# Two convolution norms' moments moved from VectorE to ScalarE, two product blocks moved from GpSimd to VectorE, and one more block folded before its transposes

## The chip, the cores and the metric

The kernel runs on one core of a Trainium2 chip. The metric is device time in microseconds of one execution, the median over runs. The core's engines run their own instruction queues in order and meet through semaphores: TensorE (PE, with its weight loads as PEld), VectorE (DVE), ScalarE (ACT), GpSimd (POOL) and the queue that issues most transfers (SP). Each engine starts an instruction only when the one ahead of it in its queue has been issued and when its own waits are met, so one late wait holds all that stands behind it.

## The reference, cut to what matters

A decoder layer with three sublayers, each followed by a residual and a layer norm, over x of 16 batches, 256 positions and 512 features:

```python
x = _layernorm(x + attention(x, w_q, w_k, w_v, w_o))          # 16 heads, causal, ternary weights
x = _layernorm(x + convolution(ctx, ctx, x, ssm_kernel, D))   # the part that is changed
x = _layernorm(x + feed_forward(x, gamma, W))                 # RMS norm, 8-bit rows, ternary W

def convolution(k, v, q, ssm_kernel, D):          # 32 heads of 8 channels, L = 512
    kv = einsum('bhil,bhjl->bijhl', k, v)         # all 64 products of two channels of a head
    y = causal_convolution(kv, ssm_kernel)        # along l, by a transform of length 1024
    out = y + kv * D
    return einsum('bijhl,bhil->bjhl', out, q)     # weighed by the queries and summed over i
```

Here k and v are both the context, so the product of channels i and j is that of j and i, and only the distances d = j - i from 0 to 4 (modulo 8, half of distance 4) have to be multiplied: 4 x 128 + 64 = 576 columns for 8 channels by 16 batches.

## The kernel before, in words

The first half of the time is attention for 16 batches, software-pipelined by `step`; nothing in it changes. The second half is the loop over the 32 heads `h` of the convolution, `for h in range(XH)` at line 1071, and a tail, `last_heads`, at line 987. Both are written out in an order by hand: the calls are made in the order in which each engine gets its instructions, so the order of the calls in the loop body is the order of every queue.

What one pass of the loop does, for head `h` and the heads before and after it:

- `load` (line 735) fetches, two heads ahead, the head's context `c` and a matrix `w` of shifted filter taps. `multiply` (line 942, through `prepare`, line 739) makes the products `kv` of head h + 1. Distance k takes columns k x 128 to (k + 1) x 128, and distance 4, half as wide, the last 64. GpSimd multiplies distances 1, 2, 4 and 3 (distance 4 together with 2); ScalarE squares for distance 0 (`square`, line 760).
- `products` (line 785) is the convolution as matrix products: position block `lb` of four takes lb + 1 blocks of taps, two halves of 288 columns each. Its result `y` fills two PSUM banks, and there are two such buffers, so a block may be computed while VectorE still reads the one before it, but not two blocks ahead. Below, P0 to P3 are the products of blocks 0 to 3.
- `with_queries` (lines 797 to 812) is VectorE's five instructions that multiply a block of `y` by the queries `q`, into `own` and `turn`. Below, Q0 to Q3.
- `add` (lines 960 and 962) is GpSimd's sum of `own` and `turn`, eight parts into four; for the blocks in `FOLDED` it then folds four parts into two. Below, A0 to A3 with F1 to F3; block 0 is not folded before the change.
- `read` (line 968, with `total` at line 817) transposes the parts of a block and sums them in PSUM into `tok`: two transposes for a folded block, four for block 0. Ten transposes a head.
- For head h - 1 the finished `tok` is normalised. `second_moments` takes mean and variance by `moments2` (line 833): `bn_stats`, `bn_aggr`, and one small instruction for each quarter of a shifted variance, all on VectorE. `engine_roots`, `newton` and `inverse_roots` (lines 843 to 863) turn a quarter into a reciprocal root, partly on ScalarE. `second_centred` and `second_max` (lines 878 and 882) prepare the 8-bit rounding; `second_norm` (line 884) makes the normalised `x2` and the rounded rows `fi`; `turn` (line 900) transposes these by a transfer.
- For head h - 2, `feed_product` (line 907) multiplies by the ternary weights and `feed_forward` (line 909) adds the residual into `r3` and takes its moments, again by `moments2`. For head h - 3, `finish` (line 914) normalises `r3` and sends it out.
- `copy` (lines 772 and 773) is ScalarE's copy of the queries of head h + 1, which Q0 of that head needs.

So VectorE's queue has, in one pass: Q0, Q1, the moments of `tok`, `second_centred`, a reciprocal, `second_max`, Q2, a reciprocal and six small instructions, `r3` and its moments, Q3. GpSimd's has A3 and F3 of the head before, distance 1, A0, distances 2 and 4, A1, F1, distance 3, A2, F2. TensorE's has P0, `read` of block 2 of the head before, P1, `read` of block 3 of the head before, P2, `feed_product`, `read` of block 0, P3, `read` of block 1.

In the tail, `last_heads`, the last head's norm, the feed-forward products of the last two heads and three output norms follow each other with nothing of the loop left to lie beside them.

Of the kernel before, what the change touches and what calls it, by code (L numbers as in the profile page):

```python
# [9 lines left out]
F32 = mybir.dt.float32  # L10
# [5 lines left out]
P = 128  # L16
# [16 lines left out]
def decoder_kernel(ctx: ExitStack, tc: tile.TileContext, x, ctx_t, w_q, w_k, w_v, w_o, ker, d_skip, gamma, w_f, out):  # L33
# [151 lines left out]
    def rounded(pool, tag, t):  # L185

        xi = pool.tile([P, E], BF16, name=f"{tag}_i", tag=f"{tag[:2]}_i")
        nc.scalar.activation(xi, t, AF.Copy, bias=-MAGIC)
        return xi
# [539 lines left out]
    with ExitStack() as l2:  # L729
# [2 lines left out]
        ps_y = l2.enter_context(tc.tile_pool(name="ps_y", bufs=2, space=PSUM, side="right"))  # L732
        pb = l2.enter_context(tc.tile_pool(name="pb", bufs=1, side="right"))
        gam = pb.tile([P, E], F32, name="gam")
        op = l2.enter_context(tc.tile_pool(name="op", bufs=4, side="right"))


# [3 lines left out]
        def prepare(h):  # L741


            c = lp.tile([P, NB, EXT, B], F32, name="c")
            nc.sync.dma_start(c[:, :, 0:XD, :], ctx_t[h])
            nc.sync.dma_start(c[:, :, XD:EXT, :], ctx_t[h][:, :, 0 : EXT - XD, :])

            w = lp.tile([P, E], F32, name="w")
            nc.sync.dma_start(w, bass.AP(taps.tensor, taps.offset + h * (E + P), [[1, P], [1, E]]))

            kv = cp.tile([P, NB, NPAIR], F32, name="kv")

            def part(at, n, i, d):
                nc.gpsimd.tensor_tensor(  # L754
                    kv[:, :, at : at + n * B].rearrange("p c (i b) -> p c i b", b=B),
                    c[:, :, i : i + n, :], c[:, :, i + d : i + d + n, :], ALU.mult,
                )

            def square():
                nc.scalar.activation(  # L760
                    kv[:, :, 0:P].rearrange("p c (i b) -> p c i b", b=B), c[:, :, 0:XD, :], AF.Square
                )

            def multiply(k):
                part(k * P, XD, 0, k)
                if k == 2:
                    part(4 * P, 4, 0, 4)

            q = cp.tile([P, NB, EXT, B], F32, name="q")

            def copy(c=slice(0, NB)):
                nc.scalar.copy(q[:, c, 0:XD, :], x1t[:, h, c])
                nc.scalar.copy(q[:, c, XD:EXT, :], x1t[:, h, c, 0 : EXT - XD, :])

            return w, kv, q, multiply, copy, square

        FOLDED = (1, 2, 3)
        Y0 = E - HALF

        def products(lb, w, kv):  # L780
# [50 lines left out]
        FORMS = ((1.0, LN_EPS), (1.0, LN_EPS), (1.0 + RMS_EPS, RMS_EPS * LN_EPS))  # L831

        def moments2(src, roots, forms):
            st = sm.tile([P, 6], F32, name="st2")
            nc.vector.bn_stats(st, src)
            mv = sm.tile([P, 2], F32, name="mv2")
            nc.vector.bn_aggr(mv, st)
            for i in forms:
                a, b = FORMS[i]
                nc.vector.tensor_scalar(roots.quarter[:, i : i + 1], mv[:, 1:2], a / 4, b / 4, ALU.mult, ALU.add)  # L840
            return mv[:, 0:1]

        def engine_roots(roots):
            c = roots.cols
            nc.scalar.activation(roots.root[:, c], roots.quarter[:, c], AF.Sqrt)  # L845
# [18 lines left out]

        def shifted(mean, res):
            shift = sm.tile([P, 1], F32, name="shift")
            nc.vector.tensor_scalar(shift, mean, res, -1.0, ALU.mult, ALU.mult)
            return shift

        def second_moments(m, roots):  # L870
# [4 lines left out]

        def second_centred(m):
            m.xn = fp.tile([P, E], F32, name="xn")
            nc.vector.scalar_tensor_tensor(m.xn, m.flat, m.mean, gam, ALU.subtract, ALU.mult)

        def second_max(m):  # L880
            m.amax = sm.tile([P, 1], F32, name="amax2")
# [2 lines left out]
        def second_norm(m, roots):  # L884
            rstd, both = (roots.res[:, i : i + 1] for i in (1, 2))
            shift = shifted(m.mean, rstd)
            m.x2 = fp.tile([P, E], F32, name="x2")
            nc.scalar.activation(m.x2, m.flat, AF.Identity, bias=shift, scale=rstd)
            amax = m.amax
            nc.vector.tensor_scalar(amax, amax, both, 1e-5, ALU.mult, ALU.add)  # L890
            mul = sm.tile([P, 1], F32, name="mul2")
            nc.vector.reciprocal(mul, amax)
            nc.vector.tensor_scalar(mul, mul, both, 127.0, ALU.mult, ALU.mult)
            m.inv = sm.tile([P, 1], F32, name="inv2")
            nc.vector.tensor_scalar(m.inv, amax, w_inv[:, 4:5], 1.0 / 127.0, ALU.mult, ALU.mult)
            m.ft = fp.tile([P, E], F32, name="fq_t", tag="q_t")
            nc.scalar.activation(m.ft, m.xn, AF.Copy, bias=MAGIC, scale=mul)
            m.fi = rounded(fp, "fq", m.ft)

        def turn(m):  # L900
            m.fit = fp.tile([P, NB, P], BF16, name="fit")
# [37 lines left out]
        def square(m):  # L939
            m.inputs[5]()  # L940

        def multiply(m, k):
            m.inputs[3](k)

        def copy(m, *blocks):
            m.inputs[4](*blocks)
# [73 lines left out]
        with tc.manual_schedule(engines=by_hand):  # L1020
            load(first_head, 0)
            load(heads[1], 1)
            nc.sync.dma_start(gam, gamma.partition_broadcast(P))
            multiply(first_head, 1)
            multiply(first_head, 2)
            acc = {0: turn_sums(m, 0)}
            divide_sums(m)
            acc[1] = turn_sums(m, 1)
            keep(k, B - 3, (1,))
            m.ots, m.last = {}, {}  # L1030
            for t in range(NT):
                divide(m, t, acc[t])
                out_scales(m, slice(t, t + 1))
                m.ots[t] = scaled(ap, f"oq{t}", m.o[:, t, :], m.mul_o[t])
                if t == 0:
                    moments(n)
            multiply(first_head, 3)
            square(first_head)
            m.oit = kp.tile([P, NT, NB, P], BF16, name="oit")
            transposed(ps, m.oit[:, 0], rounded(ap, "oq0", m.ots[0]))  # L1040
            close(m, slice(0, 1))
            transposed(ps, m.oit[:, 1], rounded(ap, "oq1", m.ots[1]))
            normalize(n)
            moments_one(m, 0)
            keep(n, B - 2, (0,))
            multiplied(first_head, 0)
            normalize_one(m, 0)
            keep(m, B - 1, (0,))
            copy(first_head, slice(0, 1))
            copy(first_head, slice(1, NB))  # L1050
            block(first_head, 0)
            close(m, slice(1, 2))
            moments_one(m, 1)
            multiplied(first_head, 1)
            block(first_head, 1)
            normalize_one(m, 1)
            keep(n, B - 2, (1,))
            multiplied(first_head, 2)
            keep(m, B - 1, (1,))
            l1.close()  # L1060
            fp = l2.enter_context(tc.tile_pool(name="fp", bufs=2))
            sm = l2.enter_context(tc.tile_pool(name="sm", bufs=3))
            ps_k = l2.enter_context(tc.tile_pool(name="ps_k", bufs=2, space=PSUM))
            ps2 = l2.enter_context(tc.tile_pool(name="ps2", bufs=2, space=PSUM))


            def roots_for(h):
                return roots_of(slice(0 if h > 2 else 1, 3))

            ahead = roots_for(0)  # L1070
            for h in range(XH):
                roots, ahead = ahead, roots_for(h + 1)

                on(load, h + 2, h + 2)
                on(add, h - 1, 3)
                on(block, h, 0)
                on(read, h - 1, 2)
                on(multiply, h + 1, 1)
                on(square, h + 1)

                on(block, h, 1)
                on(add, h, 0)
                on(read, h - 1, 3)
                on(multiply, h + 1, 2)
                on(second_moments, h - 1, roots)
                if h > 0:
                    engine_roots(roots)
                on(second_centred, h - 1)
                if h > 0:
                    newton(roots)  # L1090
                on(second_max, h - 1)

                on(block, h, 2)
                on(feed_product, h - 2)
                if h > 0:
                    inverse_roots(roots)
                on(add, h, 1)
                on(read, h, 0)
                on(multiply, h + 1, 3)
                on(second_norm, h - 1, roots)  # L1100
                on(turn, h - 1)
                on(finish, h - 3, roots, h - 3)
                on(copy, h + 1)
                on(feed_forward, h - 2, ahead)

                on(block, h, 3)
                on(add, h, 2)
                on(read, h, 1)
            last_heads(ahead)
# [37 lines left out]
```

## Time and profile before

| What | us |
|---|---|
| median of three runs (862.62 to 864.34) | 863.07 |
| the profiled execution, its own time | 861.76 |
| its span | 860.0 |
| mean granted TensorE clock | 0.988 |
| TensorE busy | 803.8 |
| VectorE busy | 690.5 |
| GpSimd busy | 583.4 |
| ScalarE busy | 427.0 |

The profiled execution's own time is the span and 1.76 us that lie around it; it is 1.31 us under the median. Busy shares over the whole span mix attention with the loop over heads. In the stretch from 500 to 800 us, which holds nothing but the loop, TensorE is 99% busy, GpSimd 93%, VectorE 88% and ScalarE 42%, and one head takes 12.40 us. A busy TensorE isn't proof of a TensorE at its limit, since matmul ends are modelled: a short wait can be hidden in a row.

In the views below, "<-" after a square bracket's number names what ended the idle time before an instruction; a group of equal instructions on one line has the time from the first one's start to the last one's end.

### The profile page before, as it was taken

The numbers are of one execution on the slowest core, as the hardware profiler recorded it, in microseconds if no ns is written. First come the engines' busy times: TensorE is split into PE (matmuls) and PEld (weight loads), VectorE is DVE, ScalarE is ACT, GpSimd is POOL, SyncE is SP. The second block draws the span as 40 slices with busy tenths as digits, with TensorE's granted clock in tenths as the row PEclk, the third lists the DMA queues.
The fourth block names the chain that finished last, engine by engine and source line by source line (L and its number), as shares of the span: only waits on it lengthen the run. The fifth ranks groups of instructions, "written<-read, shape, count | busy, mean of one in ns | idle before, by whom it ended". The sixth has DMA issues, their size and how long they took to land.

```text
span 860.0 us, 20228 instructions
## 1 busy us (share of the span) xinstructions
PE 803.8 (93%) x7754; PEld 555.9 (65%) x7754; DVE 690.5 (80%) x1889; ACT 427.0 (50%) x707; POOL 583.4 (68%) x652
## 2 busy tenths in 40 slices
PE   4889999999999999998878999999999999999993
PEld 3556666666666666665646767776777677777762
DVE  6757887788888778876666888988898889888885
ACT  6555655556565555655644334433443444344434
POOL 5265544545454454544639999999999999999980
PEclk9999999999999999999979999999999999999997
DMA  9111222333122222211320233223323332333211
GB/s 319 45 33 53 66 69 69 75 76 76 26 63 68 71 75 76 51 39 35 88 65 19 69 99 95 71 81 99 88 67 91 99 84 68 95 98 74 75 38 55
DMA packets 102207, 64.51 MB, mean 75 GB/s; under 512 B 66464, under 2 KB 83104, under 8 KB 102112
## 3 DMA queue, kind: packets, MB, share of 16 engines
q1 hardware_dynamic: 102112, 63.23, 27.5%
q8 instruction: 61, 1.00, 0.5%
q14 instruction: 34, 0.28, 0.1%
HBM read 43.34 MB, written 8.47 MB: 60 GB/s over the span
## 4 chain that ended last, share of the span: by engine, by line
PE 77%; DVE 10%; ACT 6%; issue 4%; POOL 2%; DMA 0%; ACTq 0%; DVEq 0%; POOLq 0%
PE y L785 32%; PE s L341 6%; PE acc L293 6%; PE s L381 5%; ACT p L386 4%; PE tok L820 4%; PE pv L409 4%; PE s L334 4%; PE acc_o L482 3%; DVE nmax L346 3%; PE acc_f L907 3%; PE sums L416 2%; PE s L374 2%; PE acc_v L311 2%; PE tp L528 1%
## 5 line engine op out<-in xcount | busy, mean ns | idle before, releaser
L785 PE MATMUL y<-kv,w 128*128 128x288 f32 x1280 | 335.0, 409 | 4.4 <-DVE turn L812 2.0
L785 PEld LDWEIGHTS y<-kv,w 128*128 128x128 f32 x1280 | 234.0, 191 | 64.9 <-PE tok L820 10.5
L960 POOL TENSOR_TENSOR own<-own,turn 128x512 f32<-128x512 f32 x127 | 161.7, 1274 | 21.1 <-DVE turn L812 11.0
L390 POOL TENSOR_SCALAR_AFFINE_SELECT p<-p 128x512 f32<-128x512 f32 x128 | 81.3, 659 | 139.5 <-ACT p L386 129.1
L754 POOL TENSOR_TENSOR kv<-c 128x512 f32<-128x512 f32 (+1 forms) x128 | 144.4, 1140 | 2.9 <-PE sums L416 2.9
L346 DVE TENSOR_REDUCE nmax<-s 128x4 f32<-128x512 f32 (+1 forms) x128 | 116.5, 952 | 35.5 <-PE s L341 35.5
L386 ACT ACTIVATE p<-s 128x1536 f32<-128x1536 f32 x64 | 92.9, 1452 | 70.3 <-PE s L381 70.2
L845 ACT ACTIVATE root<-quarter 128x3 f32<-128x3 f32 (+2 forms) x34 | 7.0, 204 | 159.5 <-DVE quarter L840 159.5
L396 POOL TENSOR_TENSOR both<-p 128x512 f32<-128x512 f32 x64 | 82.3, 1286 | 5.3
L797 DVE SCALAR_TENSOR_TENSOR own<-y,q 128x128 f32<-128x128 f32 x128 | 36.7, 286 | 50.5 <-PE y L785 42.6
L962 POOL TENSOR_TENSOR own<-own 128x256 f32<-128x256 f32 x95 | 69.1, 727 | 7.5
L293 PE MATMUL acc<-xit,w 128*128 128x256 bf16 x504 | 68.9, 276 | 3.6 <-DVE w L158 3.4
L800 DVE TENSOR_TENSOR own<-y,q 128x384 f32<-128x384 f32 x128 | 70.1, 548 | 0.0
L803 DVE TENSOR_TENSOR turn<-y,q 128x384 f32<-128x384 f32 x128 | 70.1, 548 | 0.0
L820 PEld LDWEIGHTS tok<-ident,own 128*128 128x128 f32 x318 | 37.7, 141 | 38.5 <-POOL own L962 26.0
L293 PEld LDWEIGHTS <-w 128*128 128x128 bf16 x512 | 45.9, 99 | 24.1 <-issue 8.5
L820 PE MATMUL tok<-ident,own 128*128 128x128 f32 x318 | 58.7, 283 | 2.4 <-issue 1.2
L341 PE MATMUL s<-kt,qt 32*128 32x128 f32 (+1 forms) x1024 | 60.0, 348 | 0.0
L381 PE MATMUL s<-qt,kt 32*128 32x256 f32 (+1 forms) x1024 | 57.4, 335 | 0.0
L409 PE MATMUL pv<-p,va 128*32 128x256 f32 (+1 forms) x1024 | 54.9, 332 | 0.0
L421 ACT COPY ot<-pv 128x256 f32<-128x256 f32 x64 | 23.9, 373 | 50.8 <-PE pv L409 50.2
L334 PE MATMUL s<-mask,ident_h 128*128 128x256 bf16 x256 | 38.3, 271 | 11.0 <-ACT p L386 9.9
(148 smaller groups left out, 1359.8 us busy)
## 6 DMA issues: line engine op xcount, KB each, us to landing
xt<-in_x SPq DMA_DIRECT2D x16, 512.0 KB, 4.1
xr<-in_x SPq DMA_DIRECT2D x16, 512.0 KB, 4.6
c<-in_ctx_t SPq DMA_DIRECT2D x32, 256.0 KB, 3.3
w<-taps SPq DMA_DIRECT2D x32, 256.0 KB, 4.1
out_y<-res SPq DMA_DIRECT2D x31, 256.0 KB, 2.3
c<-in_ctx_t SPq DMA_DIRECT2D x32, 128.0 KB, 3.2
x1t<-in_w_q SPq DMA_DIRECT2D x1, 1024.0 KB, 6.6
x1t<-in_w_k SPq DMA_DIRECT2D x1, 1024.0 KB, 9.4
```

The source lines that it names most:

```text
L293: nc.tensor.matmul(acc[:, j, :], w[:, c, o * P : (o + 1) * P], m.xit[:, c].rearrange("p t k -> p (t k)"), start=(c == 0), stop=(c == NB - 1),)
L341: nc.tensor.matmul(s[:, r, lo:hi], m.qt[rows, g, q0 : q0 + P], m.kt[rows, g, 0:nk], start=False, stop=True, skip_group_check=True,)
L346: nc.vector.tensor_reduce(m.nmax[:, t, :, g], s[:, :, cols], AX.X, ALU.max, negate=True)
L381: nc.tensor.matmul(s[:, r, lo:hi], m.kt[rows, g, k0 : k0 + P], m.qt[rows, g, q0:S], start=False, stop=True, skip_group_check=True,)
L386: nc.scalar.activation(p, s[:, :, 0 : 3 * P], AF.Exp)
L390: nc.gpsimd.affine_select(out=own, in_=own, compare_op=ALU.is_ge, fill=0.0, base=0, pattern=[[0, 4], [1, P]], channel_multiplier=-1,)
L396: nc.gpsimd.tensor_tensor(both, p[:, :, P : 2 * P], p[:, :, 2 * P : 3 * P], ALU.add)
L409: nc.tensor.matmul(acc[rows, q0:S], m.va[:, j, 4 * g + r, :], p[:, r, src], start=(j == 0), stop=(j == 1), skip_group_check=True, tile_pos ...
L754: nc.gpsimd.tensor_tensor(kv[:, :, at : at + n * B].rearrange("p c (i b) -> p c i b", b=B), c[:, :, i : i + n, :], c[:, :, i + d : i + d + ...
L785: nc.tensor.matmul(y[:, Y0 + k * HALF : Y0 + (k + 1) * HALF], lhs, kv[:, mb, k * HALF : (k + 1) * HALF], start=(mb == 0), stop=(mb == lb),)
L820: nc.tensor.matmul(tok[:, lb, :], lhsT=own[:, d, :], rhs=ident, is_transpose=True, start=(d == last), stop=(d == 0))
L960: nc.gpsimd.tensor_tensor(own[:, 0:4, :], own[:, 0:4, :], turns[lb], ALU.add)
```

## The change

Four things are changed.

- `moments2` goes from VectorE to ScalarE. Instead of `bn_stats`, `bn_aggr` and a small instruction for each quarter, ScalarE copies the row with a running sum into `total`, scales it to `minus_mean`, squares the shifted row with a running sum into `squares`, and makes each quarter by a scaled copy. This holds for both norms, the one of `tok` and the one of `r3`. Since the mean now has its sign turned, `shifted` and `second_centred` change their operation.
- Distances 3 and 4 of the products of head h + 1 go from GpSimd to VectorE: distance 3 just before `second_centred`, distance 4 just before `feed_forward`. For the first head they stay on GpSimd, distance 4 as a call of its own after distance 3.
- Block 0 is folded too. GpSimd has one more fold a head, and `read` of block 0 has two transposes instead of four.
- In `second_norm`, `x2` comes after the scaled and rounded rows on ScalarE instead of before them, and `second_max` comes ahead of `newton` in the loop; in `last_heads` it stays behind it.

```diff
+        unused = pb.tile([P, E], BF16, name="unused")
...
-            def part(at, n, i, d):
-                nc.gpsimd.tensor_tensor(
+            def part(at, n, i, d, engine):
+                engine.tensor_tensor(
                     kv[:, :, at : at + n * B].rearrange("p c (i b) -> p c i b", b=B),
                     c[:, :, i : i + n, :], c[:, :, i + d : i + d + n, :], ALU.mult,
                 )
...
-            def multiply(k):
-                part(k * P, XD, 0, k)
-                if k == 2:
-                    part(4 * P, 4, 0, 4)
+            def multiply(k, engine):
+                part(k * P, 4 if k == 4 else XD, 0, k, engine)
...
-        FOLDED = (1, 2, 3)
+        FOLDED = (0, 1, 2, 3)
...
         def moments2(src, roots, forms):
-            st = sm.tile([P, 6], F32, name="st2")
-            nc.vector.bn_stats(st, src)
-            mv = sm.tile([P, 2], F32, name="mv2")
-            nc.vector.bn_aggr(mv, st)
+            total = sm.tile([P, 1], F32, name="total2")
+            nc.scalar.activation(unused, src, AF.Copy, accum_out=total)
+            minus_mean = sm.tile([P, 1], F32, name="minus_mean")
+            nc.scalar.activation(minus_mean, total, AF.Copy, scale=-1.0 / E)
+            squares = sm.tile([P, 1], F32, name="squares")
+            nc.scalar.activation(unused, src, AF.Square, bias=minus_mean, accum_out=squares)
             for i in forms:
                 a, b = FORMS[i]
-                nc.vector.tensor_scalar(roots.quarter[:, i : i + 1], mv[:, 1:2], a / 4, b / 4, ALU.mult, ALU.add)
-            return mv[:, 0:1]
+                nc.scalar.activation(
+                    roots.quarter[:, i : i + 1], squares, AF.Copy, scale=a / (4 * E), bias=b / 4
+                )
+            return minus_mean
...
-            nc.vector.tensor_scalar(shift, mean, res, -1.0, ALU.mult, ALU.mult)
+            nc.vector.tensor_scalar(shift, mean, res, None, ALU.mult)
...
-            nc.vector.scalar_tensor_tensor(m.xn, m.flat, m.mean, gam, ALU.subtract, ALU.mult)
+            nc.vector.scalar_tensor_tensor(m.xn, m.flat, m.mean, gam, ALU.add, ALU.mult)
...
         def second_norm(m, roots):
             rstd, both = (roots.res[:, i : i + 1] for i in (1, 2))
             shift = shifted(m.mean, rstd)
-            m.x2 = fp.tile([P, E], F32, name="x2")
-            nc.scalar.activation(m.x2, m.flat, AF.Identity, bias=shift, scale=rstd)
...
             nc.scalar.activation(m.ft, m.xn, AF.Copy, bias=MAGIC, scale=mul)
             m.fi = rounded(fp, "fq", m.ft)
+            m.x2 = fp.tile([P, E], F32, name="x2")
+            nc.scalar.activation(m.x2, m.flat, AF.Identity, bias=shift, scale=rstd)
...
-        def multiply(m, k):
-            m.inputs[3](k)
+        def multiply(m, k, engine=nc.gpsimd):
+            m.inputs[3](k, engine)
...
             multiply(first_head, 3)
+            multiply(first_head, 4)
             square(first_head)
...
                 on(second_moments, h - 1, roots)
                 if h > 0:
                     engine_roots(roots)
+                on(multiply, h + 1, 3, nc.vector)
                 on(second_centred, h - 1)
+                on(second_max, h - 1)
                 if h > 0:
                     newton(roots)
-                on(second_max, h - 1)
...
                 on(read, h, 0)
-                on(multiply, h + 1, 3)
                 on(second_norm, h - 1, roots)
                 on(turn, h - 1)
                 on(finish, h - 3, roots, h - 3)
                 on(copy, h + 1)
+                on(multiply, h + 1, 4, nc.vector)
                 on(feed_forward, h - 2, ahead)
```

After the change VectorE's queue in one pass has Q0, Q1, distance 3, `second_centred`, `second_max`, a reciprocal, Q2, a reciprocal and six small instructions, distance 4, `r3`, Q3. GpSimd's has A3, F3, distance 1, A0, F0, distance 2, A1, F1, A2, F2.

## The prediction

> **What bounds the kernel now.** I read the page's groups first, then the chain that ended last through one head of the loop, then the instructions of that head in order of time, then the start of the kernel, where two engines touch the same memory. Attention (0 to 440 us) isn't touched and stays as it is. In the loop TensorE is the bound; the chain of one head is
>
> ```profile
> 607.69 2.18 PE y L785 x8
> 609.87 0.38 PE tok L820 x2
> 610.25 2.91 PE y L785 x12
> 613.17 0.86 PE acc_f L907 x4
> 614.03 0.44 PE tok L820 x4
> 614.47 3.88 PE y L785 x16
> 618.35 0.22 PE tok L820 x2
> 618.57 0.97 PE y L785 x4
> 619.54 0.42 PE tok L820 x2
> 619.96 0.13 issue
> 620.09 2.18 PE y L785 x8
> ```
>
> From one start of P1 to the next it is 12.40 us. Two transposes that wait for nothing take 0.22 (at 618.35); the four of block 0 take 0.44. The pairs at 609.87 and 619.54 take 0.38 and 0.42, because they wait for GpSimd's folds. And P1 can't start at once: it needs the buffer that Q3 of the head before it frees.
>
> ```profile
> 606.06 0.29 DVE L797 SCALAR_TENSOR_TENSOR own<-y,q 128x128 f32<-128x128 f32 x1 [0.22 <-PE y L785]
> 607.33 0.22 DVE L812 TENSOR_TENSOR turn<-y,q 128x64 f32<-128x64 f32 x1
> 607.69 1.27 POOL L960 TENSOR_TENSOR own<-own,turn 128x512 f32<-128x512 f32 x1 [0.64 <-PE tok L820]
> 610.95 1.26 POOL L960 TENSOR_TENSOR own<-own,turn 128x512 f32<-128x512 f32 x1
> 611.38 0.69 DVE L835 BATCH_NORM_STATS2 st<-tok 128x6 f32<-128x512 f32 x1
> ```
>
> Q3 starts at 606.06, as P3 ends, and ends at 607.55; P1 starts 0.14 later, at 607.69. So TensorE's period is set by the moment at which Q3 may start: whatever makes VectorE late for Q3 lengthens the head by as much. VectorE waited 0.22 there, so it has little to spare.
>
> **The frame.** I count from the end of P1 (609.87 above is 0). Before, Q3 starts at 8.59. The next P1 starts 1.63 after Q3's start, so the head's time changes by what Q3's start changes.
>
> **The change, part by part.**
>
> Folding block 0: two transposes less at 614.03, 0.22 a head. GpSimd's extra fold F0 (0.73, the row of the other folds) ends near 3.2 to 3.5; the transposes come at 4.15, after P2 and the feed-forward product. That is the cover, and 0.7 is its size. The pair at 619.54 loses its wait for GpSimd, since A2 and F2 come earlier, but P1 behind it still waits for Q3: worth nothing. Alone, this part would start Q3 at 8.37.
>
> Moments off VectorE: 0.69 + 0.18 + 0.22 for `tok` and 0.70 + 0.18 + 0.15 for `r3`, with gaps some 2.1 us a head. Distance 3 and distance 4 come on: by the 512-column TENSOR_TENSOR of line 449, 0.69, and between its rows of 64 (0.215) and 384 columns (0.548), 0.41 for 256. GpSimd loses 1.28 and 0.73 and gains 0.73. By busy time alone VectorE gains 1.0 us a head. But both products read two operands in SBUF beside a GpSimd that is never idle for long, and the start of the kernel shows what that costs:
>
> ```profile
> L158 DVE SCALAR_TENSOR_TENSOR w<-x1t,limits x2: 1285/1437/1589, 11.5 to 17.0; 128x1024 bf16<-128x1024 f32 x2
> L251 POOL TENSOR_SCALAR diag<-ident,x_v x4: 602/616/1562, 7.8 to 19.0; 128x128 f32<-128x128 f32 x4
> 15.88 1.04 DVE L157 TENSOR_SCALAR x1t<-x1t,limits 128x1024 f32<-128x1024 f32 x1
> 16.95 1.59 DVE L158 SCALAR_TENSOR_TENSOR w<-x1t,limits 128x1024 bf16<-128x1024 f32 x1
> 15.68 0.70 POOL L182 TENSOR_SCALAR xq_t<-xt,x_m 128x512 f32<-128x512 f32 x1 [6.69 <-DVE w_inv L147]
> 16.35 1.13 POOL L182 TENSOR_SCALAR xq_t<-xt,x_m 128x512 f32<-128x512 f32 x1
> 17.45 1.56 POOL L251 TENSOR_SCALAR diag<-ident,x_v 128x128 f32<-128x128 f32 x1
> ```
>
> Line 158 reads two SBUF operands. With GpSimd idle it took 1.29, issued in the middle of a GpSimd instruction 1.59; the GpSimd instruction issued behind it took 1.56 instead of 0.61. They take turns: VectorE loses what is left of GpSimd's instruction less 0.21 (0.30 of 0.53), GpSimd what is left of VectorE's less 0.14 (0.95 of 1.09).
>
> Played through with these two rules: distance 3 is issued at 1.51, where `bn_stats` was (611.38), during A0, which runs from 1.08 to 2.34 (610.95). It waits 0.62 and ends at 2.82. F0 waits for it. From that end both queues run on by known steps. GpSimd: rest of F0 0.55, distance 2 1.24, A1 1.35, F1 0.69, so A2 begins 3.82 later, at 6.64, and ends at 7.91. VectorE: `second_centred`, `second_max` and the reciprocal 1.42, Q2 with its gap 1.39, a reciprocal and six small instructions 1.14, so with a start 0.08 before distance 3's end distance 4 is issued 3.94 after it, at 6.76, which is 0.12 into A2. It waits 0.94 and ends at 8.11 instead of 7.17. `r3` follows at 8.03, Q3 at 8.69. That is 0.32 later than TensorE would allow and 0.10 later than before: the saved transposes are swallowed and a head costs 0.10 more. Bounds: without a stall at distance 4 a head gains 0.22; with distance 4 issued just as A2 begins it loses 0.12 more than I say. For 29 heads (2 to 30) +2.9, between -6.4 and +6.4. I take +2.9, since line 158 is the nearest form of instruction and both queues start from one event.
>
> The Trainium skill, "SBUF — State Buffer", section "Who interferes with whom", says that a VectorE instruction with two SBUF inputs and a GpSimd instruction that reads SBUF exclude each other for a whole instruction, and that the order of issue decides. By its letter, with no lead at either end, A2 and distance 4 would come within 0.02 of each other, and the sum would be 860 or 885; the trace's instructions let go 0.14 to 0.21 early, and I go by the trace.
>
> Moments on ScalarE: nearest rows are 0.60 (line 772, a copy) with 0.19 for reading the running sum (line 132 at the start has that second instruction), 0.20 for a small one, 0.71 (line 897, a scale by pointer) for the square. Less the 0.10 by which neighbours overlap, the root starts 2.1 us after `tok` is ready, against 1.2 on VectorE (843.76 to 844.96). In the loop that is covered: `minus_mean` is ready at 1.4 and needed at 2.7, the root at 2.7 and needed at 4.1. ScalarE's work grows from 5.2 to some 9.3 us a head; its queue of a pass ends near 12.0 of 12.5, and it could be 1.3 late before `second_centred` noticed. The copy of the queries ends at 10.2, just as Q0 wants it, and Q0 has over 1 us until P2 needs its buffer. `x2` behind the rounded rows is used a pass later; the transposing transfer on SP is issued at 8.0 as before (7.9) and used a pass later; what stands behind it on SP are the output and loads two heads ahead, which now wait for VectorE's last read of a `c` as well, a pass old by then. The changed operations of `shifted` and `second_centred` are the same instructions in the same places. P0 of the next head now waits for distance 4, at 8.11 before P3's end at 8.25.
>
> The tail has no cover. The last norm's first reciprocal waits for the root: +0.6. The rounded rows no longer wait for `x2`: -0.2. Between the rounded rows and the copy of their transposes (849.94) ScalarE now has `x2` 0.7, the earlier output 0.7 and all moments of the previous `r3`, 2.0, where only the output stood: +2.6. The last output's moments: +0.9. Sum +3.9; with small instructions at 0.38 (line 855) it would be 4.9, with everything at its shortest 3.3.
>
> The first heads: TensorE waited 0.81 for GpSimd at 471.23, and with 1.28 us less on GpSimd this goes until Q3 sets the start: -0.5 (between -0.8 and +1.3, if VectorE is late there too).
>
> Sum: +2.9 + 3.9 - 0.5 = +6.3 on the profiled 861.76, 868.1; the median of the runs stands 1.3 higher, so 869.4.
>
> **Rivals.**
>
> B, distance 4 gets in ahead of A2, or the engines don't exclude each other here. 0.12 us decides: were VectorE that much quicker between the two events, distance 4 would find F1 nearly over. Then TensorE sets the head at 12.18: -0.22 x 30 = -6.6, with the tail and the start 859.9, faster. For it speaks how thin 0.12 is; against it that line 158 shows the exclusion and that both chains of steps are read from 0.01-us rows that repeat in every head.
>
> C, ScalarE becomes the bound. It needs 1.4 us a head above my 4.1 us of new work. Even with all five small instructions at 0.38 it would be 0.9. At 2.0 above, 0.6 x 29 more: 887.
>
> D, the two take turns from head to head, so that half of the heads stall: about 864.6. Each head starts anew from Q3's end, which speaks against it.
>
> That the fold doesn't do what it says is no rival of its own: its gain is lost in my forecast already.
>
> **How the numbers follow.** My forecast 0.58, B 0.27, C 0.07, D 0.08. A measurement here can tell 0.2%, 1.7 us, from no change. My forecast's own range is 863 to 876: its stall follows A2's end one to one, and 0.2 us there is 6 us. With B the range is 858.5 to 875, which leaves out C and the ends of the two. Slower: 0.56 + 0.07 + 0.03 of D; same: 0.02 + 0.05 of B + 0.04 of D; the rest, 0.23, faster.
>
> **What would show it.** Right: in the loop a line 755 instruction of 256 columns on VectorE that takes 1.2 to 1.4 us and ends just after a line 964 one on GpSimd, the one of 512 columns near 1.3, F0 stretched to 1.0, Q3 not waiting for TensorE, heads of 12.5 us, transposes of block 0 in 0.22, `fit` copied 2.9 us later in the tail. Wrong: products of 0.4 and 0.7 and heads of 12.2 (B); VectorE waiting for `minus_mean` or the root (C).

## The result

The changed kernel takes 873.81 us (median of four runs, 872.96 to 876.14), the kernel before 863.71 (862.62 to 865.03) beside it: a ratio of 1.012, 95% interval 1.0102 to 1.0139. It is slower, by 10.1 us; the forecast was 6.3. The profiled execution has a span of 871.4 us against 860.0; that is 1.3 more of a difference, because the profiled execution lies 1.95 us under the median before and 0.64 after.

Where the 11.4 us of the two spans come from is read from the starts of P1, TensorE's products of block 1, which mark every head:

| Stretch | Before | After | Difference | Forecast |
|---|---|---|---|---|
| start to P1 of head 2 | 471.50 | 472.32 | +0.82 | -0.5 |
| 29 heads to the last P1 | 359.38 | 366.09 | +6.71 | +2.9 |
| last P1 to the end | 29.12 | 32.99 | +3.87 | +3.9 |

A head takes 12.62 us instead of 12.39 over the 29, 12.64 in the stretch shown here. TensorE now waits in every head for Q3, VectorE's five instructions on block 3. The page's row for P0 to P3 (its last field is idle time and what ended it; it was 4.4 us before) and, from the instructions of line 755, VectorE's products of distances 3 and 4 (shortest, median and longest in ns):

```profile
L784 PE MATMUL y<-kv,w 128*128 128x288 f32 x1280 | 336.6, 410 | 22.6 <-DVE turn L811 22.5
...
L755 DVE TENSOR_TENSOR kv<-c x62: 412/1404/1478, 450.0 to 834.7; 128x512 f32<-128x512 f32 x31, 128x256 f32<-128x256 f32 x31
```

The smallest, 0.41 us, is a distance 4 with nothing in its way; the longest, 1.48, is a distance 4 too. One head, in order of time; P1 ends at 600.44, which is the 0 of the frame that the prediction counts in:

```profile
601.53 1.26 POOL L964 TENSOR_TENSOR own<-own,turn 128x512 f32<-128x512 f32 x1
601.95 1.40 DVE L755 TENSOR_TENSOR kv<-c 128x512 f32<-128x512 f32 x1
602.87 1.06 POOL L966 TENSOR_TENSOR own<-own 128x256 f32<-128x256 f32 x1
607.15 1.27 POOL L964 TENSOR_TENSOR own<-own,turn 128x512 f32<-128x512 f32 x1
607.24 1.46 DVE L755 TENSOR_TENSOR kv<-c 128x256 f32<-128x256 f32 x1
608.62 0.74 DVE L915 SCALAR_TENSOR_TENSOR r<-acc_f,inv,x 128x512 f32<-128x512 f32 x1
609.28 0.27 DVE L796 SCALAR_TENSOR_TENSOR own<-y,q 128x128 f32<-128x128 f32 x1
610.90 2.18 PE L784 MATMUL y<-kv,w 128*128 128x288 f32 x8 [0.78 <-DVE turn L811]
```

Distance 3 is issued in the middle of A0 and takes 1.40; F0 behind it is stretched from 0.72 to 1.06. Distance 4, half as long, is issued 0.09 us after A2 has begun and takes 1.46: it ends 0.28 after A2. `r3` and Q3 are queued behind it, and P1 behind Q3. Before, Q3 had an idle moment of 0.22 ahead of it and waited for TensorE; now it has none.

The changed kernel has the other case as well, in the loop's second and third pass. There distance 4 is issued 0.04 and 0.05 us ahead of A2 and takes 0.41, and A2 is the one that is stretched. The third pass:

```profile
481.15 0.41 DVE L755 TENSOR_TENSOR kv<-c 128x256 f32<-128x256 f32 x1
481.20 1.49 POOL L964 TENSOR_TENSOR own<-own,turn 128x512 f32<-128x512 f32 x1
```

From the fourth pass (493 us) to the last, distance 4 is issued 0.07 to 0.09 behind A2 every time and takes 1.46 to 1.48.

In the tail, ScalarE's instructions between the last rounded rows and the copy of their transposes:

```profile
856.60 0.63 ACT L188 ACTIVATE fq_i<-fq_t 128x512 bf16<-128x512 f32 x1
857.14 0.76 ACT L902 ACTIVATE x<-tok,shift,res 128x512 f32<-128x512 f32 x1
857.80 0.80 ACT L930 ACTIVATE res<-r,shift,res 128x512 f32<-128x512 f32 x1
858.50 0.61 ACT L835 ACTIVATE unused<-r 128x512 bf16<-128x512 f32 x1
...
859.48 0.72 ACT L839 ACTIVATE unused<-r,minus_mean 128x512 bf16<-128x512 f32 x1
...
860.43 0.57 ACT L196 COPY fit<-tp 128x512 bf16<-128x512 bf16 x1
```

From the end of the rounded rows (857.23) to the copy it is 3.20 us; it was 0.69 before.

### The profile page after: what moved, and what is told of

It reads as the page before. It is cut to its first block, busy times and chain, and to the rows that moved or that the text cites. A ratio compares the mean times of both kernels' runs of the same rounds, so it can differ in the third digit from the quotient of the medians.

```text
span 871.4 us, 20354 instructions
## 1 busy us (share of the span) xinstructions
PE 792.9 (91%) x7690; PEld 551.7 (63%) x7690; DVE 703.3 (81%) x1727; ACT 548.4 (63%) x1123; POOL 559.6 (64%) x622
## 4 chain that ended last, share of the span: by engine, by line
PE 60%; ACT 16%; DVE 15%; issue 6%; POOL 2%; DMA 1%; DVEq 0%; ACTq 0%; SPq 0%; POOLq 0%
PE y L784 18%; PE s L341 6%; PE acc L293 6%; PE s L381 5%; ACT p L386 4%; PE pv L409 4%; PE s L334 4%; DVE nmax L346 3%; PE acc_o L482 3%; PE acc_f L911 3%; ACT x L902 3%; ACT fq_t L899 2%; ACT res L930 2%; PE sums L416 2%; DVE turn L802 2%
## 5 line engine op out<-in xcount | busy, mean ns | idle before, releaser
L784 PEld LDWEIGHTS y<-kv,w 128*128 128x128 f32 x1280 | 234.7, 191 | 83.8 <-PE tok L819 29.1
L966 POOL TENSOR_TENSOR own<-own 128x256 f32<-128x256 f32 x127 | 103.9, 818 | 10.0
L755 DVE TENSOR_TENSOR kv<-c 128x512 f32<-128x512 f32 (+1 forms) x62 | 85.5, 1379 | 0.0
L755 POOL TENSOR_TENSOR kv<-c 128x512 f32<-128x512 f32 x66 | 83.6, 1268 | 2.7 <-PE sums L416 2.7
L859 ACT ACTIVATE full<-quarter,root,inv_root 128x1 f32<-128x1 f32 x96 | 30.4, 377 | 50.9 <-DVE inv_root L855 50.9
L819 PEld LDWEIGHTS tok<-ident,own 128*128 128x128 f32 x254 | 33.0, 141 | 30.6 <-POOL own L966 15.3
L819 PE MATMUL tok<-ident,own 128*128 128x128 f32 x254 | 50.2, 280 | 1.6 <-POOL own L966 1.6
```

The source lines that it names most:

```text
L755: engine.tensor_tensor(kv[:, :, at : at + n * B].rearrange("p c (i b) -> p c i b", b=B), c[:, :, i : i + n, :], c[:, :, i + d : i + d + n, ...
L784: nc.tensor.matmul(y[:, Y0 + k * HALF : Y0 + (k + 1) * HALF], lhs, kv[:, mb, k * HALF : (k + 1) * HALF], start=(mb == 0), stop=(mb == lb),)
L819: nc.tensor.matmul(tok[:, lb, :], lhsT=own[:, d, :], rhs=ident, is_transpose=True, start=(d == last), stop=(d == 0))
L966: nc.gpsimd.tensor_tensor(own[:, 0:2, :], own[:, 0:2, :], own[:, 2:4, :], ALU.add)
```

## The experiments

Three theories of the longer head were set against each other. Theory 1: distance 4, with two operands in SBUF, and A2, which reads SBUF, exclude each other, and the one issued first goes first. Theory 2: VectorE has too much work ahead of Q3, or this form of instruction takes 1.4 us by itself. Theory 3: the moments on ScalarE make VectorE late. Attention, which no run changes, differs by some 4 us from execution to execution (the first P0 of head 0 starts at 441.0 to 445.5), so the heads are read from the profiles, with the medians beside them.

### Distance 4 two small instructions earlier

```diff
             nc.vector.tensor_scalar(mul, mul, both, 127.0, ALU.mult, ALU.mult)
+            if ahead is not None:
+                multiply(ahead, 4, nc.vector)
             m.inv = sm.tile([P, 1], F32, name="inv2")
...
-                on(multiply, h + 1, 4, nc.vector)
```

`ahead` is head h + 1 here; the first pass, which has no norm, keeps distance 4 in its old place.

> Edit: in the loop the distance-4 product on VectorE is issued two small instructions earlier (right behind the second small instruction that makes mul), nothing else. In the changed kernel it is issued 0.09 us after A2 has begun and takes 1.46 us. Theory 1 (the two engines exclude each other and the order of issue decides): it is now issued about 0.15 us ahead of A2, takes about 0.4 us, Q3 waits for TensorE again, a head takes 12.18 us instead of 12.62, and the median falls by 29 x 0.44 = 13 us from 873.8 to about 861. Theory 2 (VectorE simply has too much work ahead of Q3, or this form of instruction takes 1.4 us by itself): nothing but order changes, 873.8. Theory 3 (the moments on ScalarE make VectorE late): 873.8.

Measured 860.63 us, 0.9971 of the kernel before (0.9957 to 0.9985). VectorE's and GpSimd's instructions of one head, and two starts of P1 from the chain that ended last:

```profile
603.20 0.48 DVE L755 TENSOR_TENSOR kv<-c 128x256 f32<-128x256 f32 x1
603.36 1.46 POOL L966 TENSOR_TENSOR own<-own,turn 128x512 f32<-128x512 f32 x1
605.01 0.29 DVE L796 SCALAR_TENSOR_TENSOR own<-y,q 128x128 f32<-128x128 f32 x1 [0.42 <-PE y L784]
...
606.63 2.18 PE y L784 x8
618.82 2.18 PE y L784 x8
```

Now A2 is the one that is stretched, 1.46 instead of 1.27, and it makes nobody late. Distance 4 takes 0.48, Q3 waits for TensorE again, a head is 12.19 us. The same instructions on the same engine in almost the same place, with the moments on ScalarE as before: theories 2 and 3 fall here. Distance 3 still takes 1.40 in this run, so its stall alone costs the head nothing.

### Distance 4 one small instruction earlier

```diff
             nc.vector.tensor_scalar(m.inv, amax, w_inv[:, 4:5], 1.0 / 127.0, ALU.mult, ALU.mult)
+            if ahead is not None:
+                multiply(ahead, 4, nc.vector)
```

> Edit: distance 4 one small instruction earlier than in the changed kernel, which is one later than in the run that moved it by two. By the changed kernel's trace it would be issued 0.03 us ahead of A2's start, a tie. If the instruction that is issued first takes the turn: a head 12.18, the median 861, A2 stretched. If GpSimd takes its turn sooner after its start than VectorE after its issue: 873.8, a head 12.62 or, since distance 4 now comes earlier but still ends with A2, the same 12.62. A median between the two would say that heads differ.

Measured 863.01 us (0.9987, 0.9972 to 1.0002), with attention late by 3.6 us in the profiled execution. Of one head:

```profile
606.79 0.42 DVE L755 TENSOR_TENSOR kv<-c 128x256 f32<-128x256 f32 x1
606.82 1.52 POOL L966 TENSOR_TENSOR own<-own,turn 128x512 f32<-128x512 f32 x1
...
610.11 2.18 PE L784 MATMUL y<-kv,w 128*128 128x288 f32 x8 [0.33 <-DVE turn L811]
622.30 2.18 PE L784 MATMUL y<-kv,w 128*128 128x288 f32 x8 [0.33 <-DVE turn L811]
```

Issued 0.03 us ahead of A2 (0.02 to 0.05 over all heads), distance 4 takes 0.42 and the head 12.19. One small instruction, 0.12 us, decides over 0.45 us a head.

### The second operand from PSUM, twice

```diff
-                on(multiply, h + 1, 4, nc.vector)
+                on(multiply, h + 1, 4, nc.vector, heads[h - 1].tok if h > 0 else None)
```

> Edit: the distance-4 product stays in its place on VectorE with as many elements, but its second operand is read from PSUM (the tok of the head before) instead of from SBUF, so distance 4 is not computed as the reference has it. Theory 1 (exclusion of two readers of SBUF): it takes about 0.4 us instead of 1.46, a head 12.18 us, the median about 861. Theory 2 (too much work on VectorE ahead of Q3): the same number of elements on the same engine in the same place, 873.8. Theory 3 (moments on ScalarE): 873.8.

Measured 903.18 us, a miss of every theory. The instruction itself did take 0.42, but not where it was meant to:

```profile
621.87 0.42 DVE L767 TENSOR_TENSOR kv<-c,tok 128x256 f32<-128x256 f32 x1 [1.87 <-ACT x L908]
```

ScalarE's `x2` also reads `tok`, and the product waited for that read to end, although both only read. The experiment had brought a wait of its own, 1.87 us in front of Q3 (a head 13.55), and told nothing of the theories. It was repeated with an operand that no other engine reads:

```diff
+                on(multiply, h + 1, 4, nc.vector, heads[h - 2].acc if h > 1 else None)
```

> Edit: as the run with tok as the second operand of distance 4, but from another place in PSUM: the feed-forward product of head h - 2, which no other engine reads, so that no wait for ScalarE comes with it (distance 4 is again not what the reference has). Theory 1 (two readers of SBUF exclude each other): issued in its old place, after A2 has begun, it takes about 0.42 us, Q3 waits for TensorE, a head takes 12.18 us, the median is about 861. Theory 2 (the amount of work on VectorE ahead of Q3, or the form of the instruction): 873.8, a head 12.62.

Measured 861.96 us (0.998, 0.9966 to 0.9993), a head 12.18 us. In one head:

```profile
605.52 1.28 POOL L970 TENSOR_TENSOR own<-own,turn 128x512 f32<-128x512 f32 x1
605.60 0.41 DVE L767 TENSOR_TENSOR kv<-c,acc_f 128x256 f32<-128x256 f32 x1
```

Issued 0.08 us after A2 began, as in the changed kernel, it takes 0.41 and A2 (1.28) isn't stretched either. So the order of issue matters only because both operands lie in SBUF. This is theory 1 shown directly.

### Distance 4 on GpSimd again, and behind r3

```diff
                 on(multiply, h + 1, 2)
+                on(multiply, h + 1, 4)
...
-                on(multiply, h + 1, 4, nc.vector)
```

> Edit: distance 4 of all heads back on GpSimd, behind distance 2, as in the kernel before; distance 3 stays on VectorE. Theories 1 and 2: VectorE reaches Q3 1.4 us earlier, a head takes 12.18 us, median about 861; GpSimd has 0.7 more a head and still ends F2 before it is read. Theory 3 (moments on ScalarE): 873.8.

Measured 861.88 us (0.9977, 0.996 to 0.9994), a head 12.18 (P1 at 609.54 and 621.72). GpSimd had room for 0.7 us.

```diff
-                on(multiply, h + 1, 4, nc.vector)
                 on(feed_forward, h - 2, ahead)
+                on(multiply, h + 1, 4, nc.vector)
```

> Edit: in the loop r3 is issued ahead of distance 4 instead of behind it. Theory 1 (what costs is the wait of distance 4 for A2's end, 0.98 us, with r3 queued behind it): r3 (one operand in PSUM) runs in that time, distance 4 still ends at about 8.26 in the frame, but Q3 comes right behind it, at 8.2, under the 8.37 of TensorE: a head 12.18, the median about 861. Theory 2 (the amount of work ahead of Q3): the sum on VectorE is unchanged, 873.8.

Measured 862.17 us (0.9979, 0.9967 to 0.9991), a head 12.18. VectorE's instructions with A2 above them:

```profile
603.22 1.28 POOL L964 TENSOR_TENSOR own<-own,turn 128x512 f32<-128x512 f32 x1
...
603.30 0.74 DVE L915 SCALAR_TENSOR_TENSOR r<-acc_f,inv,x 128x512 f32<-128x512 f32 x1
603.96 0.82 DVE L755 TENSOR_TENSOR kv<-c 128x256 f32<-128x256 f32 x1
604.86 0.29 DVE L796 SCALAR_TENSOR_TENSOR own<-y,q 128x128 f32<-128x128 f32 x1
```

The product still waits for A2 (0.82 instead of 0.41), but `r3`, with one operand in PSUM, runs beside A2 in the meantime.

### The moments alone, and the fold alone

The kernel before with `moments2`, `shifted`, `second_centred` and `second_norm` of the changed kernel and nothing else of it:

> Edit: the kernel before with the moments of both norms on ScalarE and x2 behind the rounded rows, and nothing else (products and folds as before). My account: TensorE and the chain from P3 over Q3 to P1 set the head before, so VectorE's 2 us less are worth nothing: a head stays 12.40 us; the tail is 3.9 us longer; the median is 3 to 4 us over the kernel before, about 867.5. A rival (VectorE's relief is a gain by itself): a head under 12.35, the median at or under the kernel before.

Measured 867.89 us, 1.0042 (1.0028 to 1.0056). P1 in the chain at 610.92 and 623.32, a head 12.40; from the last P1 to the end 33.1 us instead of 29.1. VectorE's busy time in 300 us of the loop falls from 263 to 215 us, and the head doesn't move: it was not what set it.

The kernel before with `FOLDED = (0, 1, 2, 3)` and nothing else:

> Edit: the kernel before with block 0 folded too, and nothing else. GpSimd's queue then has, by start-to-start steps of the trace of before, 5 sums and products that start 1.23 apart from the next, 4 sums of 1.35, one product of 0.69 and 4 folds of 0.68: about 12.5 us a head against 12.40. Theory: GpSimd becomes the bound, a head takes 12.5 us, the median is about 3.5 us over the kernel before, 867. A rival (TensorE stays the bound): a head 12.18, the median about 857.

Measured 867.85 us, 1.0045 (1.0028 to 1.0062); P1 at 600.22 and 612.74, a head 12.52. What PE's weight loads, GpSimd's busiest follower, waited for between 500 and 800 us (us in total, times, longest):

```profile
PEld tok L820 <- POOL own L962: 30.6, 24, 1.4
```

So the fold by itself makes GpSimd the bound, at 97% busy. (The expectation's steps add up to its 12.5 us with three products 1.23 apart, which is what GpSimd has, and not with five.) The fold needs products taken off GpSimd; with the moments off VectorE, one of them, distance 3, is enough (the run with distance 4 on GpSimd).

### The tail's moments on VectorE, and a version of all that helped

Only in `last_heads` the three calls of `moments2` go back to VectorE:

> Edit: only the three moments of the tail go back to VectorE (bn_stats, bn_aggr, quarters, and one small instruction for the turned mean); the loop stays as changed. My account of the tail (3.9 us longer, from the moments on ScalarE ahead of the copy of the transposed rows and of the last root): the tail gets about 3.3 us shorter (x2 and the earlier output still stand ahead of that copy), the median about 870.4, the head stays 12.62. A rival (the tail is longer because TensorE's clock falls in a longer wait, or because x2 was moved): under 1 us.

Measured 870.6 us (1.0089, 1.0069 to 1.011); from the last P1 to the end 29.35 us instead of 32.99, the head still 12.63. So the moments make 3.64 of the tail's 3.87; the rival of the expectation, under 1 us, falls.

Then this together with distance 4 two instructions earlier, and in the tail:

```diff
-            second_norm(last, three)
-            finish(early, three, XH - 3)
+            residual = second_norm(last, three, late=True)
...
             transposed(ps2, last.fit, last.fi)
+            residual()
+            finish(early, three, XH - 3)
```

`residual` makes `x2` of the last head, which `second_norm` here leaves out.

> Edit: the changed kernel with distance 4 two small instructions earlier (the run that gave 860.6), with the tail's three moments on VectorE (the run that gave 870.6), and in the tail x2 of the last head and the earlier output behind the copy of the transposed rows. If the two costs are separate and additive: 873.8 - 13.2 - 3.2 = 857.4, and some 0.7 less for the two instructions that no longer stand ahead of the copy: 856.7, 0.8% under the kernel before. If they overlap (the tail's gain depends on the loop's phase): 859 or more.

Measured 858.37 us, 0.9938 of the kernel before (0.992 to 0.9955), the fastest of all: the two gains add up to within 1 us of the 857.4 that their sum gives. The last step gave 0.13 instead of 0.7: the copy comes 0.57 earlier behind the rounded rows, but `x2` and the output now stand ahead of the root of the last but one head on ScalarE, whose `shift` is queued on VectorE ahead of the last `r3`.

## Why the prediction was right, and what it mis-sized

**The loop.** The chain of the prediction is what the trace shows, step for step. Forecast and measured, in the frame: distance 3 issued 1.51 and 1.51, A0 from 1.08 and 1.09, A2 from 6.64 and 6.71, distance 4 issued 6.76 and 6.80, so 0.12 and 0.09 into A2, Q3 at 8.69 and 8.84. The mis-sized term is the lead by which VectorE gets its turn before GpSimd's instruction ends. From line 158 I took 0.21 (its own rows, 0.30 lost of 0.53, give 0.23); here A2 had 1.18 left and distance 4 lost 1.46 - 0.41 = 1.05, a lead of 0.13, and distance 3 (0.84 left, 1.40 - 0.69 = 0.71 lost) has the same 0.13. The two waits in one chain make Q3 0.15 later than forecast; over the head it is 0.13, and 29 times that is the 3.8 us that the loop is over the forecast. GpSimd's lead was right: F0 had 0.48 of distance 3 ahead of it and lost 0.34, 0.14. One sum of the prediction doesn't come out: VectorE's steps, 1.42, 1.39 and 1.14 from a start 0.08 ahead of distance 3's end, put distance 4 3.87 behind that end and not 3.94, so 0.05 into A2 and not 0.12. Since distance 4 ends with A2 either way, the forecast of Q3 stands, but rival B was nearer than the text says.

The Trainium skill, "SBUF — State Buffer", section "Who interferes with whom", names the mechanism: two SBUF inputs on VectorE against a GpSimd instruction that reads SBUF, the order of issue deciding. The runs here agree, with 0.41 us for the product beside A2 with one input in PSUM, 0.42 issued 0.03 ahead of A2 and 1.46 issued 0.09 behind it. By the letter of a whole instruction's block both leads would be 0; they are 0.13 and 0.14.

**Rival B**, distance 4 ahead of A2, was priced at 12.18 us a head and 859.9; made on purpose it gave 12.19 and 860.6. That some 0.1 us decides was right too.

**The fold** saves what was said, 0.22 a head, wherever Q3 and GpSimd let it: from 12.40 to 12.18 or 12.19 in six runs. In the changed kernel it is swallowed, as forecast. What the prediction says of the fold alone, that Q3 would start at 8.37, is wrong: alone it makes GpSimd the bound, 12.52.

**ScalarE** was in time: `minus_mean` at 1.35 (forecast 1.4), the root at 2.72 (2.7). Rival C didn't come. The chain that ended last does run through ScalarE in every head of the changed kernel (16% of the span, 6% before), but the same pieces of ScalarE stand in the chain of the run with distance 4 two instructions earlier, whose head is 12.19, and between 500 and 800 us of the changed kernel neither TensorE nor VectorE shows a wait for ScalarE.

**The tail** was forecast at +3.9 and measured +3.87, with +2.51 for the step ahead of the copy (forecast +2.6), +0.45 in front of it (+0.4) and +0.9 behind it (+0.9).

**The start** came out at +0.82 instead of -0.5. In the changed kernel's execution TensorE had a low granted clock while P3 of head 0 ran, in the other only earlier, up to P1 of head 0. Stretches of before and then of after (us, PE busy, granted clock, DMA share, GB/s):

```profile
440.00:450.00 10.00, 9.61 (x35) 0.68 0.02 5
453.00:456.00 3.00, 2.69 (x14) 1.00 0.00 0
```

```profile
440.00:450.00 10.00, 9.86 (x40) 0.83 0.10 26
453.00:456.00 3.00, 3.00 (x9) 0.61 0.00 0
```

P3 of head 0 takes 5.6 us there instead of 3.9. Where this dip falls wasn't tried by a run. It isn't fixed by the code: of two runs whose code is the same up to there, the one with distance 4 one instruction earlier has it in P3 of head 0 (5.74 in the timeline), the one of all that helped has not (4.05). From the first P0 to P1 of head 2 the kernel before takes 30.20 us, the changed one 31.27, and the run of all that helped, with its clock low up to P1 of head 0 only, as in the kernel before, 29.85. So with the clock alike the start gains 0.35, near the 0.5 of the forecast, and the low clock in P3 costs the changed kernel's execution some 1.4, as far as these traces show.

## What to carry to other kernels

Before moving an elementwise instruction with two SBUF operands from GpSimd to VectorE, lay the two queues beside each other from their last common event: it is not the sum of busy times that counts but which of the two is issued first, and what is queued behind the loser. If the loser stands ahead of the bounding engine's next release, move it a few instructions forward, put a PSUM-reading instruction between, or give it a PSUM operand. Work that is hidden in a loop comes back at full price in its tail, so the tail may keep the old form.

## What the runs showed of the hardware that was not expected

The order of issue is sharp: 0.02 to 0.05 us ahead of A2 is enough to go first, 0.07 to 0.09 behind is enough to wait for nearly all of it. The one that waits loses a little less than what is left of the other's instruction: 0.13 us less for VectorE behind GpSimd and 0.14 for GpSimd behind VectorE, for these instructions, which are between 0.4 and 1.4 us long; at the kernel's start, for other forms, it was 0.23 and 0.14. And an operand in PSUM takes the instruction out of the contest, but it can bring a wait of its own: 1.87 us a head where ScalarE read the same tile.
